# Selective scans: the product with B of one set of nine moves from VectorE to GpSimd, with dt u copied out through DRAM

## The chip, the cores and the metric

The kernel runs on one core of one Trainium2 chip. A core has five engines that run beside each other: TensorE (PE; its weight loads are listed as PEld), VectorE (DVE), ScalarE (ACT), GpSimd (POOL) and SyncE (SP), which here only issues DMA transfers. Each engine works through its own instructions in order. TensorE writes its results to PSUM; GpSimd and DMA work on SBUF (and DMA on DRAM). The metric is the device time of one execution in microseconds, as a median over runs.

## The reference

The program is a chain of four layers on images of 16 x 32 x 128 x 128. The change lies in the second, a deformable convolution in which a Mamba block computes the sampling offsets. For each of 18 channels d, 16 states n and two directions, along 16384 positions l, with a(d, n) negative constants:

```
u   = silu(causal_conv1d(x))                  # 18 channels
dt  = softplus(...);  B, C = linear(u)        # 16 values of B and of C per position
h[l] = exp(dt[l] * a) * h[l-1] + (dt[l] * u[l]) * B[l]     # for every d, n
y[l] = sum over n of h[l] * C[l]  +  u[l] * D
```

The second direction does the same on the flipped sequence. Each y is then gated with silu(z) and projected.

## The kernel before

`layer1_scan` works in two passes (`halves`) of eight images each, and cuts the 16384 positions into 32 chunks of 512, which makes 64 steps. A step takes one chunk from the front for the forward direction and one from the back for the backward direction. It works with 128 partitions of 8 images x 16 channels or 8 images x 16 states, and calls the groups of channels n: n = 0 holds 16 channels forward, n = 1 the same 16 backward, n = 2 the last two channels of both directions.

For the recurrence, rows are needed for image x state, one channel at a time. Four channels make a set, and `SETS` lists nine sets (n, k): four for n = 0, four for n = 1, one for n = 2. Set 7 is (1, 3). A set's turn has two halves, h = 0 and 1, of two scans each; the nine turns have eighteen halves, and `in_half` holds a table by half (0 to 17) of the smaller work that is put between.

In the turn of set i the code does, in program order:

- `decay` brings dt of a set two turns ahead from DRAM (tile `dm`) into `dd`, four loads of 256 KB on SyncE's queue, each spreading 8 rows to 128 partitions by a broadcast read. `dd` has three buffers.
- `scans` for set i: for each half one VectorE product `pd = pd * B` over 2 x 512 elements (line 914), in place in PSUM, and two scan instructions (line 919) that read `dd` from SBUF and `pd` from PSUM and write `hh`. After the set a small reduction (line 927) keeps the last state.
- `spreads` for the next set: four matmuls (line 904) with a 0/1 matrix that write `pd`, the row dt u of each channel repeated for its 16 states. `pd` has two buffers of two PSUM banks each.
- `sums` for the set before the last: four matmuls that add up h C.
- `exps` for the next set on ScalarE (line 896): dd = exp(a dd).
- `weigh` for the set before, on GpSimd (line 940): hh = hh * C over 4 x 512 elements (two instructions of half the size for set 8, line 938).

Of the work in the table these matter here: `soft_a` to `soft_f` build dt for the next step, with ScalarE for the functions and GpSimd for 128 x 512 products and sums. `soft_c` is line 842, `soft_d` 846, `soft_e` 851 with the DMA of dt to `dm` on GpSimd's queue (line 853), and `soft_f` line 858, which computes du = dt u. For n = 1 the last two fall in half 17, in the turn of set 8. `clip` (line 992, GpSimd) and `collect` (lines 979 and 982, VectorE) finish the output of the step before; in the second 16 steps of each pass `clip` runs, in the first 16 it does not. `conv`, `gate`, `delta`, `states` and `project` are matmuls.

The instructions of TensorE, VectorE, ScalarE and GpSimd are held to program order (`in_order`). SyncE's queue is not in that list: its transfers are ordered by the framework that schedules the kernel.

Of the kernel before, what the change touches and what calls it, by code (L numbers as in the profile page):

```python
# [10 lines left out]
F32 = mybir.dt.float32  # L11
# [6 lines left out]
P = 128  # L18
# [6 lines left out]
NS = 16  # L25
CH = 512
# [635 lines left out]
def layer1_scan(tc, w, tok, ymap, halves=(0, 1)):  # L662
# [8 lines left out]
    nc = tc.nc  # L671
    V, G, S = nc.vector, nc.gpsimd, nc.scalar
    NCH = L // CH
    NR = 8 * K9
    SETS = [(0, k) for k in range(4)] + [(1, k) for k in range(4)] + [(2, 0)]
    with ExitStack() as ctx:
        cp = ctx.enter_context(tc.tile_pool(name="bc", bufs=1))
# [48 lines left out]
        rp = ctx.enter_context(tc.tile_pool(name="br", bufs=3))  # L726
        yp = ctx.enter_context(tc.tile_pool(name="by", bufs=1))
        dp = ctx.enter_context(tc.tile_pool(name="bd", bufs=3, space=DRAM))
# [8 lines left out]
        def fetch(st):  # L737
# [3 lines left out]
            for dr in range(2):  # L741
# [10 lines left out]
                for dst, tap in ((xa, 3), (xb[:, 0], 1), (xb[:, 1], 2)):  # L752
                    k3 = (3, 1, 2).index(tap)
                    for p0, n, r0, t in ((0, NR, 0, tap), (NR, 24, 24 * k3, 0)):
                        lo = l0 + sg * (t - 3)
# [27 lines left out]
        def gate(st, n):  # L783
            ps = st["pz"][n] = mm()
            for dr in range(2) if n == 2 else (n,):
                m = slice(64 * dr, 64 * dr + 64) if n == 2 else slice(0, P)
                nc.tensor.matmul(
                    ps[m], wz[1 + dr if n == 2 else 0][:, m], st["xa"][dr][0:NR],
                    start=True, stop=True, tile_position=(0, m.start), skip_group_check=True,
# [65 lines left out]
        def soft_f(nx, n):  # L855
            dt = nx["soft"].pop(n)[1]
            du = nx["du"][n] = hp.tile([P, CH], F32, name=f"du{n}", tag=f"du{n}")
            G.tensor_mul(du, dt, nx["u"][n])

        def states_a(nx, i, dr):  # L860
            ps = nx["pb"][i, dr] = mm()
# [17 lines left out]
        def scale_of(n, k, r):  # L879

            return (r // 2, 16 + r % 2) if n == 2 else (n, 4 * r + k)

        def decay(st, i):
            n, k = SETS[i]
            dd = rp.tile([P, 4, CH], F32, name="dd", tag="dd")
            for r in range(4):
                m = st["dm"][n][32 * r + 8 * k : 32 * r + 8 * k + 8]
                nc.sync.dma_start(dd[:, r], m.unsqueeze(1).to_broadcast([8, NS, CH]))
            st["dd"][i] = dd

        def exps(st, i, h):
            n, k = SETS[i]
            dd = st["dd"][i]
# [4 lines left out]
        def spreads(st, i, h):  # L898

            n, k = SETS[i]  # L900
            pd = pdu.tile([P, 2, CH], F32, name="pd", tag="pd")
# [4 lines left out]

        def scans(st, i, h):
            n, k = SETS[i]
            pd, dd = st["pd"].pop((i, h)), st["dd"][i]
            if h == 0:  # L910
                st["hh"][i] = rp.tile([P, 4, CH], F32, name="hh", tag="hh")
            hh = st["hh"][i]
            bm = st["bc"][0, scale_of(n, k, 2 * h)[0]]
            V.tensor_mul(pd, pd, bm.unsqueeze(1).to_broadcast([P, 2, CH]))  # L914
            for a in range(2):
                r = 2 * h + a
                dr = scale_of(n, k, r)[0]
                s = slice(None, None, 1 - 2 * dr)
                V.tensor_tensor_scan(  # L919
                    hh[:, r, s], dd[:, r, s], pd[:, a, s],  # L920
                    st["state"][:, 4 * i + r : 4 * i + r + 1], ALU.mult, ALU.add,
                )

            if n == 2 or h == 1:
                dr, r0 = scale_of(n, k, 2 * h)[0], 2 * h if n == 2 else 0
                t = 0 if dr else CH - 1
                V.tensor_reduce(  # L927
                    st["state"][:, 4 * i + r0 : 4 * i + 2 * h + 2],
                    hh[:, r0 : 2 * h + 2, t : t + 1], AX.X, ALU.add,
                )  # L930

        def weigh(st, i):
            n, k = SETS[i]
            hh = st["hh"][i]
# [7 lines left out]
        def sums(st, i):  # L942

            n, k = SETS[i]
            hh = st["hh"].pop(i)
# [17 lines left out]
        def project(st, dr, parts):  # L963
            if 0 in parts:
                st["po"] = mm()
            po = st["po"][0:NR]
            for k in parts:
                a, b = ((wo[0], st["g"][dr]), (wo[1 + dr], st["g"][2]), (cum, st["xa"][0][0:NR]))[k]
                nc.tensor.matmul(
# [3 lines left out]
        def collect(st, dr):  # L973

            c, hb = st["c"][dr], st["hb"]
            po = st.pop("po")[0:NR]
            t = st["t"][dr] = yp.tile([NR, CH], F32, name=f"t{dr}", tag=f"t{dr}")
            if st["s"] < NCH // 2:
# [43 lines left out]
        NS9 = len(SETS)  # L1022
        slots = [(st, i) for st in steps for i in range(NS9)]

        def at(f, st, *a):
            return [(f, st, *a)] if st else []

        def in_half(t, pp, pv, st, nx):


            pe = {
                0: at(conv, nx, 2, (0,)),
                1: at(conv, nx, 2, (1, 2)),
                3: at(conv, nx, 0, (0, 1, 2)),
                5: at(conv, nx, 1, (0, 1)) + at(gate, st, 0),
                6: at(conv, nx, 1, (2,)),
                7: at(delta_a, nx, 0) + at(delta_b, nx, 0),
                8: at(project, pv, 0, (0,)),
                9: at(project, pv, 0, (1, 2)) + at(delta_a, nx, 1),
                10: at(delta_b, nx, 1),  # L1040
                11: at(delta_a, nx, 2) + at(delta_b, nx, 2),
                13: at(gate, st, 1) + at(gate, st, 2) + at(project, pv, 1, (0,)),
                14: at(project, pv, 1, (1,)),
                15: at(states_a, nx, 0, 0) + at(states_a, nx, 0, 1) + at(states_b, nx, 0),
                16: at(states_a, nx, 1, 0),
                17: at(states_a, nx, 1, 1) + at(states_b, nx, 1),
            }
            act = {
                0: at(states_c, st, 1),
                4: at(silu_u, nx, 2) + at(silu_u, nx, 0),  # L1050
                7: at(silu_u, nx, 1) + at(silu_z, st, 0),
                8: at(soft_a, nx, 0),
                9: at(soft_b, nx, 0),
                11: at(soft_a, nx, 1),
                12: at(soft_a, nx, 2),
                13: at(soft_b, nx, 1, 2),
                14: at(silu_z, st, 1) + at(silu_z, st, 2),
                16: at(states_c, nx, 0),
            }
            pool = {  # L1060
                1: at(soft_c, st, 2) + at(soft_d, st, 2),
                3: at(soft_e, st, 2) + at(soft_f, st, 2),
                5: at(clip, pp, 1),
                9: at(soft_c, nx, 0),
                11: at(soft_d, nx, 0) + at(soft_e, nx, 0),
                13: at(soft_f, nx, 0) + at(clip, pv, 0),
                15: at(soft_c, nx, 1) + at(soft_d, nx, 1),
                17: at(soft_e, nx, 1) + at(soft_f, nx, 1),
            }
            dve = {  # L1070
                1: at(gated, pv, 1),
                3: at(gated, pv, 2),
                10: at(collect, pv, 0),
                11: at(gated, st, 0),
                15: at(collect, pv, 1),
            }
            return pe.get(t, []), act.get(t, []), pool.get(t, []) + dve.get(t, [])
# [5 lines left out]
        def valid(q):  # L1083
            return 0 <= q < len(slots)

        fetch(steps[0])
        with in_order(tc, nc.tensor, V, S, G):
            for q in range(-NS9, len(slots) + 2 * NS9):
                k, i = divmod(q, NS9)
                pp, pv, st, nx, nn = (  # L1090
                    steps[k + m] if 0 <= k + m < len(steps) else None for m in range(-2, 3)
                )
                if i == 0 and st:
                    if st["s"] == 0:
                        st["state"] = yp.tile([P, 36], F32, name="state", tag="state")
                        V.memset(st["state"], 0.0)
                    else:
                        st["state"] = pv["state"]
                if i == 2 and pv:
                    recall(pv)  # L1100
                if i == 7 and nn:
                    fetch(nn)
                if valid(q + 2):
                    decay(*slots[q + 2])
                for h in range(2):
                    pe, act, rest = in_half(2 * i + h, pp, pv, st, nx)
                    if st:
                        scans(st, i, h)
                    if valid(q + 1):
                        spreads(*slots[q + 1], h)  # L1110
                    if h == 0 and valid(q - 2):
                        sums(*slots[q - 2])
                    run(pe)
                    if valid(q + 1):
                        exps(*slots[q + 1], h)
                    run(act)
                    if h == 0 and valid(q - 1):
                        weigh(*slots[q - 1])
                    run(rest)
# [1487 lines left out]
```

## Time and profile before

| | before |
|---|---|
| median of 3 runs | 16696.99 us (16661.64 to 16734.23) |
| the profiled execution: its own time | 16668.54 us |
| the profiled execution: span, mean granted TensorE clock | 16666.3 us, 0.933 |
| scans of layer 1, first and last start | 6058.3 and 10722.0 us |
| PE busy over the span | 14464.2 us (87%) |
| DVE busy over the span | 14412.7 us (86%) |
| ACT busy over the span | 12525.8 us (75%) |
| POOL busy over the span | 9711.4 us (58%) |

The profile is taken from one execution. Its page lists groups of instructions: line of the kernel, engine, operation, output and inputs, shape, count; then the busy time of the group in us and the mean of one instruction in ns; then the idle time of the engine just ahead of these instructions in us, and what ended most of it. A timeline lists instructions in order of time, neighbours of one kind merged: start and duration in us, engine, line, operation. Times in timelines count from the first instruction of the execution.

### The profile page before, as it was taken

To read this page: it belongs to the slowest core of one execution; us is meant where nothing else is said; L and a number is where in the kernel's file an instruction comes from. 1 tells how busy PE (TensorE), PEld (TensorE's weight loads), DVE (VectorE), ACT (ScalarE), POOL (GpSimd) and SP (SyncE) were. 2 spreads that over 40 slices of the span, in tenths; PEclk is the share of its full clock that TensorE was granted. 3 is DMA by queue.
4 is the path that set the end of the run, shared out by engine and by line. 5 is a ranking of instruction groups with operands and counts; after the bars stand their busy time and mean duration, and the time that the engine had idled before them with its cause. 6 is when DMAs were issued, how large, how long until landed. Compare 5 with 4: busy or idle time off the path is not lost. (4 is left out here: it accounts for less than half of the span.)

```text
span 16666.3 us, 327843 instructions
## 1 busy us (share of the span) xinstructions
PE 14464.2 (87%) x126810; PEld 5828.1 (35%) x126810; DVE 14412.7 (86%) x13784; ACT 12525.8 (75%) x25236; POOL 9711.4 (58%) x17789
## 2 busy tenths in 40 slices
PE   8998999989999888888888888899999997689966
PEld 3333333333333432222222222255555554434421
DVE  9999999999999659999999999888888886698622
ACT  8999999999999557777777777598888984466411
POOL 8999999999999457778887888500000001000012
PEclk9999999999999989999999999899899998789977
DMA  0000000000000334444454445578777876444356
GB/s 23 12 13 12 12 18 12 13 13 12 18 12 8 95 110 159 160 161 164 166 166 165 163 165 167 153 186 195 194 201 196 198 194 182 98 83 83 75 150 201
DMA packets 1347602, 1837.19 MB, mean 110 GB/s; under 512 B 161685, under 2 KB 661902, under 8 KB 1335799
## 3 DMA queue, kind: packets, MB, share of 16 engines
q1 hardware_dynamic: 1289910, 1655.23, 36.2%
q0 software_dynamic: 43840, 144.20, 2.4%
q8 instruction: 997, 16.33, 0.4%
q10 hardware_dynamic: 12288, 16.79, 0.4%
q14 instruction: 567, 4.64, 0.1%
HBM read 1497.44 MB, written 229.64 MB: 104 GB/s over the span
## 5 line engine op out<-in xcount | busy, mean ns | idle before, releaser
L235 POOL TENSOR_SCALAR Rp<-su,nv 128x128 f32<-128x128 f32 x15360 | 5406.6, 371 | 167.9 <-PE pS L241 133.0
L239 ACT ACTIVATE Ra<-su,bv 128x128 f32<-128x128 f32 x15360 | 4626.2, 390 | 406.7 <-PE pS L241 403.3
L224 DVE TENSOR_TENSOR Rd<-pu,nv 128x2048 f32<-128x2048 f32 x2176 | 4856.6, 2275 | 17.8 <-PE pS L241 16.8
L241 PE MATMUL pS<-Rd,zw 128*32 128x512 f32 x17408 | 2798.0, 606 | 378.7 <-DVE Rd L224 377.9
L919 DVE TENSOR_TENSOR_SCAN hh<-dd,state,pd 128x512 f32<-128x512 f32 x2304 | 2823.1, 1267 | 152.4 <-ACT ln L834 7.1
L940 POOL TENSOR_TENSOR hh<-hh,bc 128x2048 f32<-128x2048 f32 x512 | 2319.2, 4530 | 450.8 <-DVE state L927 439.8
L1325 POOL DMA_DIRECT2D x<-ob x64 | 92.0, 1438 | 3100.4 <-DVE ob L1324 2766.5
L904 PE MATMUL pd<-du,spread 32*128 32x512 f32 x4608 | 1340.1, 655 | 574.6 <-DVE hh L919 566.7
L896 ACT ACTIVATE dd<-dd,m_a 128x512 f32<-128x512 f32 x2304 | 1514.8, 713 | 335.3 <-DMA dd<-dm 328.9
L914 DVE TENSOR_TENSOR pd<-pd,bc 128x1024 f32<-128x1024 f32 x1152 | 1400.6, 1216 | 58.7 <-ACT bc L877 55.4
L241 PE MATMUL pS<-Rp,zw 128*32 128x512 f32 x7680 | 1314.3, 598 | 26.0 <-POOL Rp L235 25.9
L1333 ACT ACTIVATE yd<-yd,nrow 128x2048 f32<-128x2048 f32 x512 | 1238.1, 2418 | 56.7 <-DMA yd<-ymap 56.7
L1213 ACT ACTIVATE ya<-pb,nrow 128x1024 f32<-128x1024 f32 x1024 | 1196.7, 1260 | 80.6 <-PE pb L1212 80.1
L241 PE MATMUL pS<-Ra,zw 128*32 128x512 f32 x7680 | 1237.3, 601 | 0.0
L1212 PE MATMUL pb<-Y,sel 32*128 32x512 f32 (+1 forms) x5120 | 1075.3, 739 | 176.0 <-ACT ya L1213 172.8
L241 PEld LDWEIGHTS pS<-Rd,zw 128*32 128x32 f32 x17408 | 582.1, 109 | 1484.7 <-DVE Rd L224 927.4
L904 PEld LDWEIGHTS pd<-du,spread 32*128 32x128 f32 x4608 | 371.1, 189 | 1607.4 <-DVE hh L919 726.8
L1217 DVE TENSOR_SCALAR yd<-yd 128x2048 f32<-128x2048 f32 x512 | 727.5, 1421 | 207.0 <-ACT yd L1333 205.8
L1217 DVE TENSOR_SCALAR ya<-ya 128x2048 f32<-128x2048 f32 x512 | 759.0, 1482 | 10.7 <-ACT ya L1213 9.4
L1224 PE MATMUL pd<-ya,xt 128*32 128x128 f32 x16384 | 691.4, 311 | 42.5 <-DVE ds L1377 31.7
L1945 PE MATMUL ps<-t,W 128*128 128x512 f32 x1280 | 635.4, 644 | 80.9 <-DVE W L1925 53.1
L1224 PEld LDWEIGHTS pd<-yd,xt 128*32 128x32 f32 x16384 | 533.2, 178 | 471.0 <-issue 224.7
(434 smaller groups left out, 22927.2 us busy)
## 6 DMA issues: line engine op xcount, KB each, us to landing
dd<-dm SPq DMA_DIRECT2D x2304, 256.0 KB
yd<-ymap SPq DMA_DIRECT2D x512, 1024.0 KB
xq<-x SPq DMA_DIRECT2D x48, 1088.0 KB
dm<-dt POOLq DMA_DIRECT2D x192, 256.0 KB, 3.8
w<-d SPq DMA_DIRECT2D x512, 73.1 KB
xb<-tok SPq DMA_DIRECT2D x248, 144.0 KB
x<-in_x SPq DMA_DIRECT2D x64, 512.0 KB
x<-o SPq DMA_DIRECT2D x128, 256.0 KB
```

What stands on the lines that cost most here:

```text
L224: nc.vector.tensor_tensor(R, st["pu"].unsqueeze(1).to_broadcast([P, 4, 4, HW]), nv[:, :, i::32].rearrange("p t q -> p q t").unsqueeze(3).t ...
L235: nc.gpsimd.tensor_scalar(R[:, q, k], su[:, k], 3.4028234e38, nv[:, k, c], ALU.min, ALU.max)
L239: nc.scalar.activation(R[:, q, k], su[:, k], AF.Relu, bias=bv[:, k, c])
L241: nc.tensor.matmul(st["pS"][32 * q : 32 * q + 32], zw[:, 31 - i : 63 - i], R[:, q], start=first, stop=False, tile_position=(0, 32 * q), sk ...
L896: S.activation(dd[:, r], dd[:, r], AF.Exp, scale=acol[:, dr, d : d + 1])
L904: nc.tensor.matmul(pd[:, a], spread[e, k], st["du"][n][e], start=True, stop=True)
L914: V.tensor_mul(pd, pd, bm.unsqueeze(1).to_broadcast([P, 2, CH]))
L919: V.tensor_tensor_scan(hh[:, r, s], dd[:, r, s], pd[:, a, s], st["state"][:, 4 * i + r : 4 * i + r + 1], ALU.mult, ALU.add,)
L940: G.tensor_mul(hh, hh, st["bc"][1, n].unsqueeze(1).to_broadcast([P, 4, CH]))
L1217: V.tensor_scalar(t, t, 1.0, 1.0, ALU.min, ALU.subtract)
L1224: M(pd[32 * q : 32 * q + 32, i], xt[:, :, xc], h, start=True, stop=True, tile_position=(0, 32 * q),)
L1333: S.activation(yd, yd, AF.Abs, bias=nrow)
```

## The change

The product with B of set 7 is computed by GpSimd ahead of time, from a copy of du in SBUF.

- `soft_f`, for n = 1, also writes du to DRAM (tile `um`, two buffers) by a DMA on GpSimd's queue.
- `brought`, in the turn of set 1, loads the eight rows of each of the four channels of set 7 into an SBUF tile `db` (one buffer of 4 x 512 elements), each repeated for 16 states by a broadcast read: four transfers on SyncE's queue.
- `inputs`, in half 7 of the table (the turn of set 3, after the product with C of set 2), multiplies `db` by B on GpSimd, 4 x 512 elements in one instruction.
- `scans`, for set 7, leaves out the two products on VectorE and hands `db` to the scan instructions in place of `pd`.
- `spreads`, in the turn before, is left out for set 7.

```diff
+    BY_POOL = 7
...
             G.tensor_mul(du, dt, nx["u"][n])
+            if n == SETS[BY_POOL][0]:
+                nx["um"] = dp.tile([P, CH], F32, name="um", tag="um", bufs=2)
+                G.dma_start(nx["um"], du)
+
+        def brought(st):
+            k = SETS[BY_POOL][1]
+            db = st["db"] = rp.tile([P, 4, CH], F32, name="db", tag="db", bufs=1)
+            for r in range(4):
+                m = st["um"][32 * r + 8 * k : 32 * r + 8 * k + 8]
+                nc.sync.dma_start(db[:, r], m.unsqueeze(1).to_broadcast([8, NS, CH]))
+
+        def inputs(st):
+            db = st["db"]
+            bm = st["bc"][0, SETS[BY_POOL][0]]
+            G.tensor_mul(db, db, bm.unsqueeze(1).to_broadcast([P, 4, CH]))
...
-            pd, dd = st["pd"].pop((i, h)), st["dd"][i]
+            dd = st["dd"][i]
+            pd = st["db"][:, 2 * h : 2 * h + 2] if i == BY_POOL else st["pd"].pop((i, h))
...
-            bm = st["bc"][0, scale_of(n, k, 2 * h)[0]]
-            V.tensor_mul(pd, pd, bm.unsqueeze(1).to_broadcast([P, 2, CH]))
+            if i != BY_POOL:
+                bm = st["bc"][0, scale_of(n, k, 2 * h)[0]]
+                V.tensor_mul(pd, pd, bm.unsqueeze(1).to_broadcast([P, 2, CH]))
...
+                7: at(inputs, st),
...
+                if i == 1 and st:
+                    brought(st)
...
-                    if valid(q + 1):
+                    if valid(q + 1) and (i + 1) % NS9 != BY_POOL:
                         spreads(*slots[q + 1], h)
```

## Prediction

> **What bounds the kernel now.** I read the page first: of the lines the change touches, all lie in the scan stage (VectorE's scans start at 6058.3 us and end at 10722.0 us, by the answer on their line), so the page's shares of the whole span say little and the stage has to be read by itself.
>
> ```profile
> L919 DVE TENSOR_TENSOR_SCAN hh<-dd,state,pd 128x512 f32<-128x512 f32 x2304 | 2823.1, 1267 | 152.4 <-ACT ln L834 7.1
> L940 POOL TENSOR_TENSOR hh<-hh,bc 128x2048 f32<-128x2048 f32 x512 | 2319.2, 4530 | 450.8 <-DVE state L927 439.8
> L914 DVE TENSOR_TENSOR pd<-pd,bc 128x1024 f32<-128x1024 f32 x1152 | 1400.6, 1216 | 58.7 <-ACT bc L877 55.4
> ```
>
> The scans wait for almost nothing, and GpSimd's product with C waits for VectorE's state. Next, the busy times of one whole step of nine sets (step 40 of 64, found by counting scans):
>
> ```profile
> core 0: us, PE busy (x) PEld busy (x) DVE busy (x) ACT busy (x) POOL busy (x), PEclk, DMA share, GB/s
> 8976.45:9048.03 71.58, 62.55 (x222) 16.57 (x223) 69.10 (x71) 52.85 (x75) 57.52 (x26) 0.98 0.48 164
> ```
>
> VectorE works 69.1 of 71.6 us and sets the pace; GpSimd is second with 57.5 us. The timeline of VectorE and then of GpSimd shows the turn of the ninefold loop that is changed (set 7, from 9032.02 us):
>
> ```profile
> 9032.02 1.22 DVE L914 TENSOR_TENSOR pd<-pd,bc 128x1024 f32<-128x1024 f32 x1
> 9033.37 2.45 DVE L919 TENSOR_TENSOR_SCAN hh<-dd,state,pd 128x512 f32<-128x512 f32 x2
> 9035.74 1.21 DVE L914 TENSOR_TENSOR pd<-pd,bc 128x1024 f32<-128x1024 f32 x1
> 9037.05 2.45 DVE L919 TENSOR_TENSOR_SCAN hh<-dd,state,pd 128x512 f32<-128x512 f32 x2
> ...
> 9040.23 1.22 DVE L914 TENSOR_TENSOR pd<-pd,bc 128x1024 f32<-128x1024 f32 x1
> ```
>
> ```profile
> 9000.67 4.52 POOL L940 TENSOR_TENSOR hh<-hh,bc 128x2048 f32<-128x2048 f32 x1 [3.69 <-DVE state L927]
> 9008.27 4.52 POOL L940 TENSOR_TENSOR hh<-hh,bc 128x2048 f32<-128x2048 f32 x1 [3.07 <-DVE state L927]
> 9017.85 1.26 POOL L842 TENSOR_TENSOR e<-e,p 128x512 f32<-128x512 f32 x1 [5.06 <-ACT p L838]
> ...
> 9031.60 1.29 POOL L858 TENSOR_TENSOR du<-dt,u 128x512 f32<-128x512 f32 x1
> 9032.84 4.53 POOL L940 TENSOR_TENSOR hh<-hh,bc 128x2048 f32<-128x2048 f32 x1
> 9037.33 1.27 POOL L842 TENSOR_TENSOR e<-e,p 128x512 f32<-128x512 f32 x1
> 9038.68 1.26 POOL L846 TENSOR_TENSOR ln<-ln,e 128x512 f32<-128x512 f32 x1
> ```
>
> While set 7 is scanned GpSimd has no gap: the end of a product du, the product with C of set 6, and two 128x512 ops of the softplus. Its gaps lie earlier: 3.07 us before the product with C of set 3, 5.06 us after it.
>
> The row that decides comes from other stages: what VectorE does when both its inputs lie in SBUF while GpSimd works. Three answers on single lines (min/median/max ns), then the timeline of the last stage at 16212 us:
>
> ```profile
> L919 DVE TENSOR_TENSOR_SCAN hh<-dd,state,pd x2304: 1252/1268/1282, 6058.3 to 10722.0; 128x512 f32<-128x512 f32 x192
> L266 DVE TENSOR_TENSOR mT<-pmm,hT x128: 673/678/685, 29.0 to 5575.4; 128x512 f32<-128x512 f32 x128
> L260 DVE TENSOR_TENSOR G<-G,aa x128: 673/759/924, 81.9 to 5579.4; 128x512 f32<-128x512 f32 x128
> ```
>
> ```profile
> 16212.20 0.68 DVE L2245 TENSOR_TENSOR pt<-pt 128x512 f32<-128x512 f32 x1
> 16212.43 4.82 POOL L2327 TENSOR_TENSOR xn<-xn,xs 128x2048 f32<-128x2048 f32 x1 [21.37 <-DVE xn L2326]
> 16212.80 5.00 DVE L2245 TENSOR_TENSOR pt<-pt 128x512 f32<-128x512 f32 x1
> 16217.73 0.68 DVE L2245 TENSOR_TENSOR pt<-pt 128x512 f32<-128x512 f32 x1
> ```
>
> L266 reads one input from PSUM and is steady; L260, the same shape with both in SBUF, takes up to 924 ns beside GpSimd. L2245, also both in SBUF, takes 0.68 us alone and 5.00 us when GpSimd's 128x2048 op, the shape of L940, is running: it ends 0.55 us after that op. GpSimd's op, begun during the first L2245, ends 4.37 us after it. The two exclude each other and take turns. Today's scan reads pd from PSUM and keeps 1252 to 1282 ns beside a busy GpSimd. After the change the scans of set 7 read dd and db, both in SBUF.
>
> **The change part by part, per step.**
>
> Removed from VectorE: two products of 1.216 us with the gap of about 0.1 us behind each. With no other effect the four scans of set 7 take 4.9 us (two pairs of 2.45) where the rows need 7.5, a gain of 2.6 us.
>
> Removed from TensorE: four spreads in the turn of set 6. TensorE waited for VectorE before them (566.7 us in all by the answer on line 904), so nothing is gained.
>
> Added to GpSimd: `inputs`, one 128x2048 product, 4.53 us like L940, between the products with C of sets 2 and 3; and the copy of du into `um` on its queue, priced as L853: 0.58 us after 0.30 us of waiting for du. Behind `inputs` stand the product of set 3 and then L842. Set 2's product ends at 9005.19, so `inputs` ends at 9009.7, set 3's at 9014.3, and L842 starts at 9017.85 as before, since ScalarE's p is last there. The 0.9 us ahead of set 8's product goes into the same gaps. Cost nothing; if the 5.06 us gap were gone, 1.5 us of lag.
>
> Added to SyncE: four loads of 256 KB at 0.62 us of issue each, 2.5 us. In 6700 to 10500 us SyncE stood 1668.6 us waiting for VectorE's state to free dd, 32 us a step. The load waits for `um`: du ends at 9047.85, L853's copies land 3.8 us after issue (median, 8.4 at most), so near 9052; the decay loads it shares the queue with are due when a turn ends, at 9048 and 9056. Issued even behind the latter it would be out at 9061 and land near 9065 by the same 3.8 us; `inputs` wants it at 9077 (9005.19 plus one step), 12 us later. The 1.25 MB are 11% of a step's 11.7 MB, with the DMA engines 48% busy. Nothing.
>
> Added to VectorE: the exclusion. No row shows a scan with two SBUF inputs. Its bounds are today's scan (no wait at all, the gain of 2.6 us) and L2245 (every scan waits for a whole GpSimd op in turn). I take the second, because it is the same engine pair, the same GpSimd op and the same kind of operands. Sizes from that row: a scan behind a GpSimd op ends 1.27 - 0.13 = 1.14 us after it (0.68 became 0.55); a GpSimd op behind a scan ends 0.16 us sooner than its own length after it (4.53 became 4.37). Set 7 then runs: du's rest 0.87 (9032.02 to 9032.89), scan 1.14, product of set 6 4.37, scan 1.14, L842 1.11, scan 1.14, L846 1.11, scan 1.14: 12.02 us, and 0.73 us for state and `collect` as now (9039.50 to 9040.23): 12.75 where it is 8.21, so **+4.54 us**. In the 32 steps of the second halves of the two passes GpSimd also has `clip` (L992, 1.98 us by its group's mean) ahead of that product; its 1.82 us takes a turn and L846 falls behind the last scan: 0.87 + 1.14 + 1.82 + 1.14 + 4.37 + 1.14 + 1.11 + 1.14 = 12.73, **+5.25 us**. GpSimd is held about 1 us per scan, and carries 57.5 + 5.4 + 4 = 67 us in a step of some 76: it does not become the bound.
>
> [...]
>
> Sum: 32 x 4.54 + 32 x 5.25 = 313 us. Off that, waits that the longer turn covers: `collect` waits for TensorE 45.7 us in the stage (26.6 and 19.1, groups of L982 and L979), a few of 7.1 us; of what lies between nothing and all of it I credit 33. Net **+280 us**: 16668.5 + 280 = 16949 against the profiled execution, which lies 28 us under the median; on the median of 16697, **16977 us**.
>
> **Rivals.**
>
> (a) Scans are not excluded. For: no row shows one, and they consume slower than a tensor_tensor. Against: L260 and L2245 differ from them in nothing else that reads SBUF. -2.6 x 64 = -166: 16531 us. Faster.
>
> (b) VectorE, once in, keeps GpSimd out over all four scans. Only du's rest is waited for: 0.87 + 1.14 + 3 x 1.22 + 0.73 = 6.4 instead of 8.2, -1.8 x 64 = -115: 16582 us, faster. Against: GpSimd's 4.82 us op got in between two neighbouring L2245. If pairs hold together (the third scan being on the queue of its own half), 0.87 + 1.14 + 1.18 + 4.37 + 1.14 + 1.18 + 0.73 = 10.6, +2.4 x 64 - 33 = +121: 16818. It decides from one GpSimd turn per set on: with one it is about even, with three it is my forecast.
>
> (c) The copy through DRAM comes late and `inputs` stops GpSimd's queue. It would have to be over 12 us late, for instance by an unlucky place in SyncE's queue, whose order is not written out by hand. Another 5 us a step: 17297 us.
>
> **How the numbers follow.** Forecast 0.83, (a) 0.06, (b) with all four scans 0.05, (c) 0.04, a mixture near zero 0.02. The range goes from pairs kept together less the spread of runs below the median (16818 - 35 = 16783) to the sum without overlap and without credit plus the spread above (16697 + 377 + 37 = 17111). It leaves out (a), (b) and (c), 15 in 100, and a little of the forecast. A change within 0.5%, 83 us, is about what measuring this kernel cannot tell from none. Faster 0.11, same 0.04, slower 0.85.
>
> **What would show it.** Right: eight ninths of the scans keep 1.27 us, those of set 7 spread up to about 5.5 us; GpSimd's L940 and 128x512 rows gain a tail about 1.1 us longer; set 7's turn is near 13 us, and the other eight are unchanged. Wrong: a scan maximum of 1.3 us ((a)); one long scan a set ((b)); waits of GpSimd on the loads of db ((c)).

## The result and the profile after

The changed kernel takes **17177.5 us** (median of 4 runs, 17153.5 to 17261.3) where the kernel before took 16689.2 us beside it (median of 4): a ratio of **1.030, 95% interval 1.026 to 1.034**. That is +488 us where +280 was forecast, and it lies above the range. The direction was right, the size was not.

The scan stage, from the first scan's start to the last scan's end, grew from 4665.0 to 5160.8 us in the profiled execution (+496); its span is 17151.8 us at a mean granted clock of 0.906 (0.933 before). The page's groups after:

```profile
L937 DVE TENSOR_TENSOR_SCAN hh<-dd,state,pd 128x512 f32<-128x512 f32 x2048 | 2510.4, 1268 | 175.7 <-PE py L971 50.9
L958 POOL TENSOR_TENSOR hh<-hh,bc 128x2048 f32<-128x2048 f32 x512 | 2321.8, 4535 | 496.0 <-DVE state L945 476.1
L912 ACT ACTIVATE dd<-dd,m_a 128x512 f32<-128x512 f32 x2304 | 1534.8, 715 | 782.3 <-DMA dd<-dm 735.2
L937 DVE TENSOR_TENSOR_SCAN hh<-dd,state,db 128x512 f32<-128x512 f32 x256 | 844.6, 3357 | 3.9 <-POOL du L859 1.6
```

The 2048 scans that still read `pd` from PSUM keep 1268 ns. The 256 of set 7 take 3357 ns on average: the exclusion is there. But GpSimd's product with C keeps its 4.53 us; the tail of 1.1 us that was forecast for it is all but absent (4 of 512 take over 5 us). Of the 128 x 512 rows the second softplus op, L847, has the tail: 62 of its 192 take about 2.07 us. How the scans of set 7 are spread, in the answer on that line (min/median/max ns):

```profile
L937 DVE TENSOR_TENSOR_SCAN hh<-dd,state,pd x2048: 1252/1269/1284, 6060.9 to 11220.5; 128x512 f32<-128x512 f32 x187
L937 DVE TENSOR_TENSOR_SCAN hh<-dd,state,db x256: 1251/2211/14815, 6129.1 to 11212.1; 128x512 f32<-128x512 f32 x128
```

The forecast had all four scans held, for up to 5.5 us. By their place in the set the medians are 8.51, 2.22, 1.25 and 1.25 us: **one long scan, one held by about 1 us, two free**. The timeline shows it for step 23 (set 6 ends at 7928.10 us). VectorE, from two short windows, the first scan by itself and then the other three:

```profile
7928.31 9.47 DVE L937 TENSOR_TENSOR_SCAN hh<-dd,state,db 128x512 f32<-128x512 f32 x1
...
7937.71 4.57 DVE L937 TENSOR_TENSOR_SCAN hh<-dd,state,db 128x512 f32<-128x512 f32 x3
```

GpSimd in the same stretch:

```profile
7927.84 1.27 POOL L859 TENSOR_TENSOR du<-dt,u 128x512 f32<-128x512 f32 x1
7929.09 1.93 POOL L1010 TENSOR_SCALAR yo<-t 72x512 f32<-72x512 f32 x1
7930.99 4.49 POOL L958 TENSOR_TENSOR hh<-hh,bc 128x2048 f32<-128x2048 f32 x1
7935.45 1.25 POOL L843 TENSOR_TENSOR e<-e,p 128x512 f32<-128x512 f32 x1
7936.78 2.06 POOL L847 TENSOR_TENSOR ln<-ln,e 128x512 f32<-128x512 f32 x1
```

The scan is issued at 7928.31 and waits through du, `clip`, the product with C and the first softplus op (L843), four instructions that start back to back. It gets in at 7936.70, where the second softplus op (L847) needs the result of the first and the records show a gap of 0.08 us. Now L847 is held (2.06 us for 1.27), and the second scan waits for that one. The hand-over is not instruction by instruction.

Next I counted, for each step, each set's turn from the end of one set's last scan to the end of the next one's (mean of steps 1 to 62, us):

| turn | 0 | 1 | 2 | 3 | 4 | 5 | 6 | 7 | 8 | step |
|---|---|---|---|---|---|---|---|---|---|---|
| before | 7.86 | 8.21 | 8.29 | 7.60 | 7.60 | 8.23 | 8.20 | 7.68 | 9.02 | 72.69 |
| after | 7.62 | 8.20 | 8.71 | 8.35 | 8.45 | 9.12 | 8.20 | 13.53 | 8.40 | 80.59 |

Turns 7 and 8 together grew by 5.23 us, 335 us over 64 steps. Turns 0 to 6 grew by 2.66 us, **170 us**, and that was in no term of the forecast. Their medians have hardly moved (8.60 in turn 2, else as before): the time lies in about ten steps in which turns 2 to 5 take some 15 us more. Windows over the whole steps 7 and 25, then over a 40 us piece of step 25, show how such a step differs:

```profile
6610.45:6686.69 76.24, 62.50 (x220) 16.84 (x216) 73.98 (x68) 53.66 (x76) 63.35 (x27) 0.93 0.49 170
8044.51:8136.68 92.17, 79.55 (x215) 20.38 (x215) 75.61 (x68) 54.21 (x76) 67.17 (x29) 0.72 0.55 164
...
8060.00:8100.00 40.00, 40.00 (x78) 10.16 (x74) 27.12 (x27) 20.58 (x28) 20.36 (x6) 0.50 0.66 171
```

Columns as in the prediction. Step 25 has the same work and 16 us more; TensorE's granted clock is 0.72 in it, and 0.50 in the piece, where TensorE is busy all of the time (40.00 of 40.00 us) and VectorE two thirds. The TensorE timeline has the same four matmuls at both clocks:

```profile
8087.33 2.08 PE L920 MATMUL pd<-du,spread 32*128 32x512 f32 x4
...
8103.16 1.13 PE L920 MATMUL pd<-du,spread 32*128 32x512 f32 x4
```

There are 10 stretches of half clock longer than 20 us after the change (41 to 44 us each, 416 us in all, every one beginning in turn 1 and ending in turn 5) against 6 before (20 to 34 us, 164 us in all, none beginning in turn 1). All half-clock time in the stage went from 423 to 1369 us; most of the rest lies in the turns of sets 7 and 8 (308 and 360 us), during and behind a pause of TensorE (median of the longest in each step 9.0 us, before 0.4):

```profile
7943.12 3.42 PE L878 MATMUL mm<-u,wb 128*128 128x512 f32 x4 [10.83 <-DVE t L1000]
```

VectorE's waits from 6700 to 10500 us (line waited for: us, times, longest) now name TensorE ahead of the products with B and of the scans, where before it stood mainly ahead of `collect` (18.1 and 10.4 us):

```profile
DVE pd L932 <- PE pd L920: 54.5, 30, 2.9
DVE hh L937 <- PE py L971: 33.3, 23, 2.8
DVE g L978 <- PE py L971: 26.4, 28, 2.1
```

### The profile page after: what moved, and what is told of

It is laid out like the page before. It is cut to its first block, busy times and chain, and to the rows that moved or that the text cites. A ratio compares the mean times of both kernels' runs of the same rounds, so it can differ in the third digit from the quotient of the medians.

```text
span 17151.8 us, 327154 instructions
## 1 busy us (share of the span) xinstructions
PE 14600.8 (85%) x126298; PEld 5879.6 (34%) x126298; DVE 14802.3 (86%) x13656; ACT 12538.0 (73%) x25236; POOL 10093.4 (59%) x17917
## 5 line engine op out<-in xcount | busy, mean ns | idle before, releaser
L937 DVE TENSOR_TENSOR_SCAN hh<-dd,state,pd 128x512 f32<-128x512 f32 x2048 | 2510.4, 1268 | 175.7 <-PE py L971 50.9
L920 PE MATMUL pd<-du,spread 32*128 32x512 f32 x4096 | 1249.4, 687 | 366.8 <-DVE hh L937 359.7
L932 DVE TENSOR_TENSOR pd<-pd,bc 128x1024 f32<-128x1024 f32 x1024 | 1246.8, 1218 | 121.4 <-PE pd L920 84.9
L878 PE MATMUL mm<-u,wb 128*128 128x512 f32 x512 | 384.8, 870 | 572.1 <-DVE t L1000 302.7
L937 DVE TENSOR_TENSOR_SCAN hh<-dd,state,db 128x512 f32<-128x512 f32 x256 | 844.6, 3357 | 3.9 <-POOL du L859 1.6
L920 PEld LDWEIGHTS pd<-du,spread 32*128 32x128 f32 x4096 | 335.8, 197 | 1319.6 <-DVE hh L937 653.0
```

The source lines that it names most:

```text
L920: nc.tensor.matmul(pd[:, a], spread[e, k], st["du"][n][e], start=True, stop=True)
L937: V.tensor_tensor_scan(hh[:, r, s], dd[:, r, s], pd[:, a, s], st["state"][:, 4 * i + r : 4 * i + r + 1], ALU.mult, ALU.add,)
```

## The experiments

Ratios are to the kernel before on the same chip, with 95% intervals; they can differ from the quotient of the two medians by up to 0.001. The medians of the kernel before were 16736.6 us beside e1 to e4, 16707.0 beside e0 and e5 to e7, 16793.0 beside e8 to e10 and 16729.1 beside e11. Where an expectation gives 16689 for the kernel before, that is its median beside the result above.

### Is the time of turns 2 to 5 the clock's?

e2: the changed kernel, with full-size products (128 rows, 128 columns, 512 wide) that are overwritten at once, so that TensorE has more to do early in the step.

```diff
             ps = nx["pu"][n]
+            if 0 in ks:
+                nc.tensor.matmul(ps, dg[0], spread.rearrange("p k m -> p (k m)"), start=True, stop=True, skip_group_check=True)
```

> The changed kernel with three more 128x128 by 128x512 products per step on TensorE, one ahead of each first conv product of the next step (halves 0, 3 and 5), overwritten by it. [...] Rival (the half clock is a consequence of waits that lie elsewhere, or TensorE has no room for 3.3 us more a step): 17170 to 17300 us, with the long turns still there.

Measured: 17064.8 us, 1.0203 [1.0182, 1.0224]. Long stretches 10 to 1; turns 2 to 5 are 8.42, 7.63, 7.61, 8.23, as before the change. The stage fell to 5029.5 us, less than the 170 us of the table, because turn 7 rose to 14.29: GpSimd is later there, and 52 times in the stage (15 times after the change) a waiting scan is passed over by du behind a product with C, so it waits out the end of that product too. With the stretches gone turns 2 to 5 have their old length: half clock is the cause of the extra 170 us. Adding work to TensorE made the changed kernel faster.

The unchanged new kernel, run again beside the next group:

> The changed kernel again, beside the kernels of this group on the same chip. All theories: 1.026 to 1.034 times the kernel before; the stretches of half clock of 41 us in some ten steps again.

Measured: 17184.4 us, 1.0281 [1.0249, 1.0313], with 12 long stretches (478 us), 10 of them again from turn 1 to turn 5, mostly in other steps. That there are about ten is a property of the kernel, not of one execution.

Which steps get them can be read from the clock records of the traces. Within the stage every change of the granted clock, in each run, lies within 5 ns of a grid of 3.413 us: the long stretches that begin at 7963.13, 8058.70 and 8150.86 us are 28 and 27 grid intervals apart. A stretch longer than 20 us begins in turn 1 where the step stands at two places on this grid: the end of set 0's last scan lies 1.3 to 1.6 or 3.06 to 3.24 us ahead of the next grid point. These bounds were read off the same runs. Counting steps 1 to 62 of each run (e1, e3, e4, e8 and e9 are described below):

| steps with such a stretch | before | after | e0 | e1 | e3 | e4 | e8 | e9 |
|---|---|---|---|---|---|---|---|---|
| of those at the two places | 0 of 1 | 10 of 10 | 9 of 11 | 14 of 16 | 1 of 1 | 4 of 5 | 8 of 8 | 2 of 4 |
| of the others | 0 of 61 | 0 of 52 | 1 of 51 | 0 of 46 | 0 of 61 | 0 of 57 | 0 of 54 | 0 of 58 |

In the six runs with extra products (e2, e5, e6, e7, e10, e11) 45 steps stand at those places, and none has such a stretch. The usual step before is 71.58 us long, 20.97 grid intervals, so that each step stands almost where the last one stood (0.11 us off by the median), and only one came to those places. After the change a step moves by 0.83 us (median), and ten came there. The pause of TensorE in turns 7 and 8 is not needed: e1 does not have it (median 0.6 us) and has 14 such steps. No run moved a step on the grid and changed nothing else.

e5: the kernel **before** with the extra products of e2 (halves 0, 3 and 5) and one more in half 10 (into the bank that `delta_a` of n = 2 then fills).

```diff
...
+        def ahead(nx):
+            ps = nx["pt"][2] = mm()
+            nc.tensor.matmul(ps, dg[0], spread.rearrange("p k m -> p (k m)"), start=True, stop=True, skip_group_check=True)
...
-                10: at(delta_b, nx, 1),
+                10: at(delta_b, nx, 1) + at(ahead, nx),
...
```

> The kernel before with four more full-size (128x128 by 128x512) products per step on TensorE, three ahead of the first conv products (halves 0, 3, 5) and one after delta_b in half 10, all overwritten. Theory (stretches of half clock are ended or kept away by full-size products, and cost time wherever they fall): the six stretches over 20 us of the kernel before go, and with them most of the difference between its mean step of 72.7 us and its usual one of 71.6: 0.995 to 0.998 of before (-35 to -80 us). Rival (TensorE has no room for 4.4 us more a step): 1.005 and more.

Measured: 16641.8 us, 0.9957 [0.9944, 0.9970]: **faster than both kernels**, by 0.4% against the kernel before. One long stretch, 195 us of half clock, stage 4640.4 us. The windows of e5 show its clock:

```profile
6060.00:7400.00 1340.00, 1210.06 (x4256) 329.61 (x4256) 1284.35 (x1281) 982.60 (x1377) 1068.90 (x464) 0.99 0.49 163
7400.00:8800.00 1400.00, 1265.49 (x4418) 343.12 (x4418) 1327.86 (x1327) 1021.08 (x1427) 1164.33 (x516) 0.98 0.51 164
```

In the same two windows the kernel before has 0.94 and 0.96, the changed one 0.88 and 0.85.

### What the exclusion is

e8: a dependent product of two columns on GpSimd behind du of n = 0, which makes GpSimd wait for its own result there.

```diff
             G.tensor_mul(du, dt, nx["u"][n])
+            if n == 0:
+                g = yp.tile([P, 2], F32, name="tiny", tag="tiny")
+                G.tensor_mul(g, du[:, 0:2], du[:, 2:4])
```

> The changed kernel with one tiny product of two columns on GpSimd after the product du of n = 0 (the op before the product with C of set 6), which reads that du, so that GpSimd has to wait for its own result there for about 0.1 us. In the changed kernel the first scan of set 7 got in only after the third or fourth GpSimd op, at the first place where GpSimd waited for itself (softplus, lines 843 to 847). [...] Theory B (a scan is served only when GpSimd's queue has run dry of ready work): the first scan stays at 7.5 to 9.5 us. The time stays within 0.5% of the changed kernel either way.

Measured (one run, no interval): 17164.9 us beside 16793.0 before, 1.022, a little further from the changed kernel than the 0.5% expected. Scans by place: medians 1.87, 1.25, 5.46, 2.22 us; the long wait fell to the third scan. The median of turn 7 fell from 13.25 to 11.18 us. One step of e8, GpSimd and then, from short windows, VectorE's first, third and fourth scan:

```profile
8014.36 1.29 POOL L859 TENSOR_TENSOR du<-dt,u 128x512 f32<-128x512 f32 x1
8015.73 1.00 POOL L862 TENSOR_TENSOR tiny<-du 128x2 f32<-128x2 f32 x1
8016.71 2.93 POOL L1013 TENSOR_SCALAR yo<-t 72x512 f32<-72x512 f32 x1
8019.62 4.50 POOL L961 TENSOR_TENSOR hh<-hh,bc 128x2048 f32<-128x2048 f32 x1
8024.09 2.17 POOL L843 TENSOR_TENSOR e<-e,p 128x512 f32<-128x512 f32 x1
```

```profile
8012.85 3.89 DVE L940 TENSOR_TENSOR_SCAN hh<-dd,state,db 128x512 f32<-128x512 f32 x1
...
8017.84 7.36 DVE L940 TENSOR_TENSOR_SCAN hh<-dd,state,db 128x512 f32<-128x512 f32 x1
...
8025.13 2.21 DVE L940 TENSOR_TENSOR_SCAN hh<-dd,state,db 128x512 f32<-128x512 f32 x1
```

The first scan got in at the new gap (0.08 us, 8015.65 to 8015.73), not 7 us later: here too VectorE got in where GpSimd waited. But that is not all. The third scan waited through the rest of `clip` and the product, and got in between the product and L843, where no gap shows; in 59 of 59 steps a scan that waited there got in (50 times the third, 9 times the second). In the changed kernel a waiting scan was passed over at that same boundary 58 times and let in 5 times. What set those boundaries apart was not shown.

e9: the scans of set 7 replaced by plain products of the same operands.

```diff
+                if i == BY_POOL:
+                    V.tensor_mul(hh[:, r, s], dd[:, r, s], pd[:, a, s])
+                    continue
                 V.tensor_tensor_scan(
```

> The changed kernel with the four scans of set 7 replaced by plain products of the same two SBUF operands (that set's states are left out). If the scan as an instruction is what lets GpSimd through several ops, the products take turns with GpSimd's ops: none over 5.3 us, most of 0.7 to 1.9 us. [...]

Measured (one run): 16956.7 us. The four products by place: 8.04, 1.75, 0.68, 0.68 us (medians); turn 7 has a median of 11.56 us. The first waits like the first scan, so it is the operands and GpSimd's row of instructions that decide, not the scan.

e1: GpSimd still makes set 7's product, but TensorE brings it into `pd` with an identity matrix, and the scans read PSUM.

```diff
...
+                if i == BY_POOL:
+                    nc.tensor.matmul(pd[:, a], eye, st["db"][:, 2 * h + a], start=True, stop=True)
+                    continue
...
-            pd = st["db"][:, 2 * h : 2 * h + 2] if i == BY_POOL else st["pd"].pop((i, h))
+            pd = st["pd"].pop((i, h))
...
```

> The changed kernel, but TensorE copies the finished product of set 7 (db times B, made by GpSimd as in the change) into pd by four products with the identity, in the places where the spreads stood; the scans of set 7 read pd from PSUM again. GpSimd's and the DMA's additions stay, VectorE's two products stay away. Theory 1 (two SBUF inputs exclude VectorE while GpSimd works, and the half clock follows from TensorE's idle time in that turn): all scans near 1.27 us, set 7's turn near 5.6 us, no stretch of half clock of 41 us; 16689 - 150 = 16540 us (16490 to 16600). Theory 2 (the loss comes from the added transfers and GpSimd work, which delay queues): it stays above 16690, up to 17100 us.

Measured: 16956.3 us, 1.0138 [1.0114, 1.0162]. The exclusion is gone: turn 7 has a median of 5.19 us. The gain is not kept. Turn 8 takes 11.23 us, and VectorE's timeline shows where: four scans without a break, then `collect` waits for TensorE.

```profile
9263.58 4.79 DVE L941 TENSOR_TENSOR_SCAN hh<-dd,state,pd 128x512 f32<-128x512 f32 x4 [1.99 <-PE py L975]
...
9271.30 0.69 DVE L1001 SCALAR_TENSOR_TENSOR t<-mm,rowpat 72x512 f32<-72x512 f32 x1 [2.74 <-PE mm L991]
```

There are also 15 long stretches of half clock (638 us), 14 of them from turn 1 to turn 5, though turns 7 and 8 have almost none (1 us in all).

### Are VectorE's 2.6 us worth anything, and are the additions free?

e4: the kernel before without VectorE's product for set 7, nothing in its place.

```diff
-            V.tensor_mul(pd, pd, bm.unsqueeze(1).to_broadcast([P, 2, CH]))
+            if i != 7:
+                V.tensor_mul(pd, pd, bm.unsqueeze(1).to_broadcast([P, 2, CH]))
```

> The kernel before without VectorE's two products with B for set 7 (that set's states are computed without B); nothing is added. It prices what the change takes off VectorE. Theory 1: 2.6 us a step, 16689 - 166 = 16523 us (16490 to 16560). Rival (TensorE, 85% busy, sets the pace as soon as VectorE is shorter): a gain of under 80 us, 16610 us or more.

Measured: 16813.5 us, 1.0049 [1.0026, 1.0071], where 166 us less were expected. Turn 7 fell to 4.94 us (median), and turn 8 rose from 8.41 to 10.80; 15 long stretches (464 us) are the likely rest, since e7, which has one, does not lose. VectorE's waits in e4:

```profile
DVE t L983 <- PE mm L970: 107.9, 28, 8.5
DVE t L980 <- PE mm L970: 56.2, 25, 2.3
```

e7: e4 with the four extra products of e5, so that the clock is out of it.

```diff
...
+            if i != 7:
+                V.tensor_mul(pd, pd, bm.unsqueeze(1).to_broadcast([P, 2, CH]))
...
+                10: at(delta_b, nx, 1) + at(ahead, nx),
...
```

> The kernel before without VectorE's product with B for set 7 (left out of the result), with the same four extra products. Without them it was 1.0049 of before. If the 2.6 us a step are lost to the half clock alone, they come back: 0.988 to 0.993. If TensorE's own work between the turns of sets 5 and 8 takes them back (collect waits for it), only the long stretches are won: 0.995 to 0.999.

Measured: 16633.7 us, 0.9955 [0.9941, 0.9969], the same as e5, which does the product. So with the clock kept up, leaving that work out gains nothing measurable: the wait of `collect` for TensorE takes most of it back (63.6 and 56.2 us in the same window, against 12.0 and 9.1 in e5).

e3: the additions alone, with VectorE's product kept and GpSimd's not used.

```diff
-            pd = st["db"][:, 2 * h : 2 * h + 2] if i == BY_POOL else st["pd"].pop((i, h))
+            pd = st["pd"].pop((i, h))
...
-            if i != BY_POOL:
+            if True:
...
-                    if valid(q + 1) and (i + 1) % NS9 != BY_POOL:
+                    if valid(q + 1):
```

> The kernel before with the additions of the change and nothing removed: the copy of du to DRAM, the four loads, and GpSimd's product with B, whose result is not used; VectorE's products, the spreads and the scans of set 7 are as before. Theory 1 (the additions are hidden, as the prediction had it): 16689 us within 50. Theory 2 (they are what costs): +150 to +490 us, 16840 to 17180 us.

Measured: 16832.4 us, 1.0066 [1.0045, 1.0087]. They are not free. Scans wait for the exponentials (1.9 us before in the same window), and SyncE's queue stands at the first load of `db` until `um` has landed:

```profile
DVE hh L937 <- ACT dd L912: 41.5, 38, 3.0
```

```profile
SPq L869 <- DMA um<-du: 421.3, 47, 14.4
```

ScalarE waited 588.4 us for the loads of `dd` (250.3 before). Half clock is up too (12 long stretches, 338 us); the 0.66% was not divided between the two.

e6: e1 with the four extra products.

```diff
...
+                if i == BY_POOL:
+                    nc.tensor.matmul(pd[:, a], eye, st["db"][:, 2 * h + a], start=True, stop=True)
...
+                10: at(delta_b, nx, 1) + at(ahead, nx),
...
```

> The kernel of the first group in which TensorE brings set 7's finished product back to PSUM, with the same four extra products. Theory (what that kernel lost were 15 long stretches at half clock, some 14 us each, and VectorE's gain is taken back by collect, which waits for TensorE): from 1.0138 to 0.995 to 1.003 of before. Rival (its loss is the added transfers and GpSimd work): stays above 1.010.

Measured: 16736.6 us, 1.0015 [0.9999, 1.0030]: no change that can be told from none. Turn 7 is 5.38, turn 8 11.24, turns 2 and 3 8.89 and 8.08 us.

### Can the idea be made to pay?

e10: e6 with `collect` of the second direction one half later.

```diff
-                15: at(collect, pv, 1),
+                16: at(collect, pv, 1),
```

> The kernel in which TensorE brings the product back to PSUM, with the four extra products, and with collect of the second direction half a turn later (half 16 in place of 15), behind the first scans of set 8. Theory (VectorE's saved time is lost in collect's wait for TensorE): the wait shrinks, turns 7 and 8 together fall from 16.6 us by 1 to 2.4 us a step, 0.992 to 0.998 of before. Rival (TensorE's work in those turns sets the pace wherever collect stands): 0.9995 to 1.003 as without the move.

Measured: 16743.3 us, 0.9970 [0.9957, 0.9983]: it beats the kernel before, by less than e5 does without moving any work. Turn 8 fell to 9.30 us; the next wait took part of it, for the exponentials, again behind SyncE's wait:

```profile
DVE hh L948 <- ACT dd L920: 91.4, 72, 4.9
```

e11: e10 with the four loads of `db` in turns 0 to 3 and `inputs` in half 9.

```diff
...
-                if i == 1 and st:
-                    brought(st)
+                if i < 4 and st:
+                    brought(st, i)
...
```

> The kernel before this one (product of set 7 on GpSimd, brought back to PSUM by TensorE, four extra full-size products, collect half a turn later), with the four loads of db issued one each in the turns of sets 0 to 3 in place of all four in the turn of set 1, and GpSimd's product with B moved from half 7 to half 9, into its 5 us gap. Theory (what is left of the additions' cost is that their 1 MB delays dd, so that ScalarE's exponentials and then the scans of sets 2 and 3 are late, some 100 us in the stage): those waits shrink to a third or less, and the ratio falls from 0.997 to 0.990 to 0.994. Rival (the bytes cost wherever they are put, the DMA engines being busy): 0.996 to 0.999.

Measured: 16751.1 us, 1.0008 [0.9998, 1.0017]: missed. SyncE's waits there still name `um`:

```profile
SPq L879 <- DMA um<-du: 616.4, 49, 17.4
```

Spreading the bytes did not help. That the waiting load at the head of the queue is what delays the decay loads fits e3, e10 and e11, but no run took that wait away by itself.

## Why the prediction was wrong

**The exclusion: right that it exists, mis-sized.** The prediction took from L2245 that the two engines "exclude each other and take turns" and gave each GpSimd op one scan. The runs show instead that the first scan waits out a whole row of GpSimd ops and the later ones are nearly free. Where GpSimd has no `clip` in that row, the total comes out almost alike: turns 7 and 8 of the first-half steps grew by 4.41 us where the sum has 4.54, or 4.02 after its credit of 33 us (0.52 a step). That does not confirm the taking of turns: the same four GpSimd ops and four scans stand one behind the other in either order. In the second-half steps, with `clip` in the row, the prediction let L846 fall behind the last scan; in fact VectorE got in just ahead of that op, held it, and waited for it once more. They grew by 6.05 us, against 5.25, or 4.73 after the credit. The term measured 335 us net, not 280; with the clock of turns 2 to 5 kept up turns 7 and 8 stand at 22.69 us (e2) against 16.41 (e5), 402 us.

**"The other eight are unchanged": the step that failed.** The prediction found nothing to pay or gain in TensorE ("so nothing is gained") and never asked what the granted clock would do. In ten steps the clock falls to half in turn 1 and stays there for 41 to 44 us, with TensorE as the pace-setter. That is the 170 us. Neither the spreads that TensorE lost nor its pause of some 9 us is needed for this: e1 has four products in place of the spreads, no such pause, and 14 such steps. By the table above it goes with the place of a step on the grid of 3.413 us, and so with the length of the steps, which the change altered; what in the work of turns 0 and 1 lets the clock fall there stays open. That the clock does fall was to be seen before: the step of the prediction's own window stands at PEclk 0.98, and the profile of before has six long stretches. How many steps would come to a bad place was not in the prediction's rows. Together the two terms miss 55 + 170 = 225 us by the mean of steps 1 to 62, times 64; the medians miss by 208.

**"Cost nothing", the additions.** In e3 they cost 0.66%. In the changed kernel itself the long turn 7 seems to cover most of that: in e2, which has them all, turns 0 to 6 and 8 are no longer in sum than before (64.3 against 65.0 us, and 64.8 in e5). So this step was wrong as a price and did little to the result.

**The gain of 2.6 us** in rivals (a) and (b) was wrong as well. Turn 7 does fall to 4.9 or 5.2 us without the exclusion (e1, e4), but turn 8 gives it back (11.23 us in e1 and 10.80 in e4, against 8.41), because TensorE's products for `collect` come no sooner. By e7 leaving VectorE's products out was worth about zero with the clock kept up, not -166 us; rival (a) should have been "no change" at best (e6 is at 1.0015, and e1, without the extra products, at 1.0138).

**The rivals themselves.** (a) and (b) are refuted by the first scan's 8.51 us; (b) had its sign come true, one long scan a set, and one thing right, that VectorE, once in, needs little more. (c) did not happen as foreseen: GpSimd waited 5.7 us in all for `db`. The late transfer stopped SyncE's queue instead (374.7 us of waiting for `um` from 6700 to 10500 us).

That GpSimd and a scan hold each other up almost fully is in the trace: behind L843 a scan that had waited ended 1.09 us later (median of 62, with 1.25 us alone), and L847 ended 1.06 us behind that scan (1.27 alone). The upper end of the range counts hand-overs without any overlap, 64 us more; no run shows such hand-overs, and these two overlapped by 0.16 and 0.21 us. A waiting scan is also passed over by further GpSimd instructions, three in step 23 (7928.31 to 7936.70 us).

## What to carry to other kernels

Here an operand that moved from PSUM to SBUF put VectorE behind GpSimd for a whole row of instructions (the first scan of set 7 takes 8.51 us by the median, a free one 1.25); count the GpSimd ops up to its next wait, not one per VectorE instruction. Before a change that alters the length of a step, look at TensorE's granted clock step by step: here stretches at half clock cost half as much as the exclusion itself (170 against 335 us), and three or four useless full-size products per step made both kernels faster (1.0203 in e2 against 1.0281 in e0, 0.9957 in e5). A saving on the busiest engine can be lost to what it waits for next (e7, without VectorE's products for set 7, is at 0.9955 and e5, with them, at 0.9957): leave the work out once and look at the next turn.

## What the runs showed of the hardware

- In step 25 TensorE was busy, as the profile counts it, for 40.00 of 40.00 us at a granted clock of 0.50, in one of ten stretches of half clock of 41 to 44 us, all of which end in turn 5. That full-size products end them is not shown: this one has a pair of 128 x 128 products (L966, 8070.15 us) in its middle. With extra full-size products none began in turn 1 in the 45 steps that stood at the places where 48 of 56 have one without them. Whether their size or only the added load did it was not shown.
- Within the stage the granted clock changed on a grid of 3.413 us (each of the 14 traces, within 5 ns), and with the place of a step on it went whether a stretch of half clock of over 20 us began in turn 1: in 48 of 56 steps at two places, in 1 of 440 elsewhere, in the eight runs without extra products.
- After the change GpSimd passed a waiting scan over at back-to-back boundaries (58 times of 63 between the product with C and L843) and let it in where it waited itself for 0.08 us (62 times of 62 between L843 and L847). Why layer 0's L260 (673 to 924 ns before, 674 to 923 after) and the scans of e8 ahead of L843 are let in sooner is not known.
- SyncE's queue stood at a load that waited for a transfer of GpSimd's queue (`um`): 375 us of 3800 after the change, up to 635 in e10.
